# Asking for the square of a Mamba block's result one block later

## The chip, the cores and the metric

The kernel runs on one core of one Trainium2 chip. The time is the device time of one execution in microseconds, taken three times; 4633.89 us is the median.

## The reference, cut to what matters

Two layers over 32 graphs of 512 nodes with 256 features. Each layer normalises, adds an attention over the graph's edges, normalises again and adds a second part: in layer 0 a Mamba-2 block over the 512 nodes, in layer 1 an LSTM along the node axis with two running sums. The lines that the change concerns are the end of the Mamba block:

```python
Y = (Y_diag + Y_off + xh * D[:, None]).reshape(Bsz, L, D_INNER)
Y = Y * jax.nn.silu(z)
Y = Y * jax.lax.rsqrt(jnp.mean(Y * Y, axis=-1, keepdims=True) + EPS) * norm_w
out = Y @ W_out
return out @ W_lin + b_lin
```

`D_INNER` is 512. The mean of `Y * Y` goes over all 512 channels of a node.

## The kernel before, in words

Everything but the LSTM is done graph by graph ("batch" below), by generators that each issue a few instructions and then yield. Several of them run side by side, shifted against each other: `mamba` on graph b, `mamba_in` and `mamba_dt` for the next one, `plain1` (the second attention, then `after1`, which stores the graph's result) on the graph before, `plain0` (the first attention) and `after0` (its normalisation) on graphs ahead. A loop at the end of `layers_per_batch` takes the generator whose due time comes first, so the code gives an order in which work is asked for. A scheduler then decides where each instruction stands in its engine's queue.[...] In the last two batches a further generator, `recurrence_weights`, prepares the LSTM's weights: POOL scales them in one tile `rwt`, SP's queue stores it to `wr`, and the next use of the tile (L1069, a memset of its last two columns) waits for that store. Four of the first eight stores have 128 rows and four have 127 (L1140). After the batches comes the LSTM (`recurrence`, 512 steps).

The Mamba block holds its 512 channels as four blocks (cc = 0 to 3) of 128 partitions by 512 nodes. For each block

- `decayed(cc)` makes g, the decay matrix of two heads: eight ACT operations (L760), one ACT exp over all of it (L764), one DVE product with C·B (L765). It is called one block ahead.
- PE adds up py from g and the inputs (L829), and from the carried states (L835).
- `finish(cc, py)` makes y = xh·D + py on DVE (L816), multiplies it by silu(z) (L817; on POOL for blocks 0 to 2, on DVE for block 3), and squares it on ACT into zs (L818). The tile zs held silu(z), which the square overwrites.

After the four blocks PE multiplies y by the joined output weights (po, L847), sums the squares (pss, L854), ACT copies the sums (ssr, L856), PE turns them into a column (psc, L859), DVE and POOL make the reciprocal root of it (L861, L54 and L56 through the helper `rstd_of`), and DVE adds the result into x (L865).

Beside this run, at the end of a batch: the last sums and results of `plain1` (pov L962, its scale rinv L967 and L969, ov L970 on ACT), `after1` (em: L874 on DVE, exp L875 on ACT; L877 and L878 on DVE; the store to X at L879), `after0` of another graph (L351 on ACT, L353 and L355 on DVE, L54, L56, L356 and L357 on POOL), and the layer norms of the next graphs: xn for `plain0` and xm for `mamba_in` (statistics L65 and L66, the offset L69 on DVE, the scaling L71 on ACT), their transposes pxT and pmT on PE (L279), and the copies of these on ACT (L282). POOL adds beta (L494) and blin (L605) to x once the norm has read it. At the start of a batch POOL multiplies ce by cT (L746) and adds bias0 to o (L593), which DVE reads at L341 before it makes xdt (L783); POOL then makes xdd (L793).

Of the kernel before, what the change touches and what calls it, by code (L numbers as in the profile page):

```python
# [13 lines left out]
AF = mybir.ActivationFunctionType  # L14
# [12 lines left out]
NC = DI // P  # L27
# [48 lines left out]
def layers_per_batch(ctx, tc, c, a, X3, odd=None, wr=None):  # L76
# [6 lines left out]
    nc = tc.nc  # L83
# [7 lines left out]
    def bank(name, pool=psr):  # L91
        return pool.tile([P, 512], F32, tag="bank", name=name)
# [589 lines left out]
    def mamba(b, state):  # L682
# [11 lines left out]
        zs = two.tile([P, NC, N], F32, tag="wide", bufs=4 if odd is not None else 3, name=f"zs{b}")  # L694
# [4 lines left out]
        xh = two.tile([P, NC, N], F32, tag="wide", bufs=4 if odd is not None else 3, name=f"xh{b}")  # L699
# [49 lines left out]
        def decayed(cc):  # L749


            bc = two.tile([P, 2, N], F32, tag="bc", name=f"bc{b}_{cc}")
            nc.sync.dma_start(
                out=bc.rearrange("p h l -> p (h l)"),
                in_=line[:, 2 * cc * N : 2 * (cc + 1) * N].to_broadcast([P, 2 * N]),
            )
            g = two.tile([P, NT, 2, P], F32, tag="g", name=f"g{b}_{cc}")
            for i in range(NT):
                for k in range(2):
                    nc.scalar.activation(  # L760
                        g[:, i, k, :], bc[:, k, i * P : (i + 1) * P], AF.Relu,
                        bias=cs[:, i, 2 * cc + k : 2 * cc + k + 1], scale=-1.0,
                    )
            nc.scalar.activation(g, g, AF.Exp, scale=-1.0)  # L764
            nc.vector.tensor_tensor(  # L765
                g, g, pcb.rearrange("p (i l) -> p i l", i=NT).unsqueeze(2).to_broadcast([P, NT, 2, P]), ALU.mult
            )
            return g
# [45 lines left out]
        def finish(cc, py):  # L814
            y = xh[:, cc, :]
            nc.vector.scalar_tensor_tensor(y, y, dcol[:, cc, :], py, ALU.mult, ALU.add)  # L816
            (nc.gpsimd if cc + 1 < NC else nc.vector).tensor_tensor(y, y, zs[:, cc, :], ALU.mult)  # L817
            nc.scalar.activation(zs[:, cc, :], y, AF.Square)  # L818

        for cc in range(NC):  # L820
            if cc + 1 < NC:
                ahead.append(decayed(cc + 1))
                yield
            g = ahead.pop(0)
            py = bank(f"py{b}_{cc}")
            for i in range(NT):
                for k in range(2):
                    h = 2 * cc + k
                    nc.tensor.matmul(  # L829
                        py[k * HD : (k + 1) * HD, i * P : (i + 1) * P],  # L830
                        xdt[:, i, h * HD : (h + 1) * HD], g[:, i, k, :],
                        start=(i == 0), stop=False,
                    )
            for i in range(1, NT):
                nc.tensor.matmul(  # L835
                    py[:, i * P : (i + 1) * P], came[:, i - 1, cc].rearrange("p two e -> p (two e)"), ce[:, cc, (i - 1) * P : i * P],
                    start=False, stop=(i == NT - 1),
                )
            finish(cc, py)
            yield  # L840
        pos = []
        for j in range(NT // 2):
            po = bank(f"po{b}_{j}")
# [158 lines left out]
    def each(*parts):  # L1002
        return stream([(b + at, b + until, make, b + n) for b in range(-2, nb + 1) for at, until, make, n in parts])

    streams = [
        each((0.0, 1.0, mamba, 0)),
        each((-0.097, -0.039, mamba_in, 0), (-0.026, 0.192, mamba_dt, 0)),
        each((0.55, 0.857, second, -1), (0.857, 1.52, first, 2)),
# [471 lines left out]
```

## Time and profile before

| what | value |
|---|---|
| three timed runs | 4614.34, 4633.89, 4634.27 us |
| their median | 4633.89 us |
| profiled execution, its own time | 4607.25 us |
| its span, first to last instruction | 4605.5 us |
| PE, DVE, ACT, POOL busy | 3910.5, 3345.0, 2957.3, 1275.3 us |
| mean granted clock of PE | 0.959 |
| starts of two ssr copies (L856), batches 5 and 6 | 672.01, 769.76 us |
| the same, batches 29 and 30 | 3020.75, 3154.71 us |
| first LSTM product | about 3303 us |

"Busy" is the time in which an engine executes. A group's or line's idle time is the idle time of the engine directly before those instructions, put down to the one whose signal came last. Idle time of an engine matters only if somebody later waits for what it did late. The granted clock is the share of full speed that PE was allowed. One batch takes about 97.5 to 98.4 us, so its end can be read on any of them; batch 5 is used, whose ssr copy starts at 672.01 us. A matmul on 32-bit data shows as two rows of the trace.

### The profile page before, as it was taken

To read this page: it belongs to the slowest core of one execution; us is meant where nothing else is said; L and a number is where in the kernel's file an instruction comes from. 1 tells how busy PE (TensorE), PEld (TensorE's weight loads), DVE (VectorE), ACT (ScalarE), POOL (GpSimd) and SP (SyncE) were. 2 spreads that over 40 slices of the span, in tenths; PEclk is the share of its full clock that TensorE was granted. 3 is DMA by queue.
4 is the path that set the end of the run, shared out by engine and by line. 5 is a ranking of instruction groups with operands and counts; after the bars stand their busy time and mean duration, and the time that the engine had idled before them with its cause. 6 is when DMAs were issued, how large, how long until landed. Compare 5 with 4: busy or idle time off the path is not lost. (4 is left out here: it accounts for less than half of the span.)

```text
span 4605.5 us, 116255 instructions
## 1 busy us (share of the span) xinstructions
PE 3910.5 (85%) x46798; PEld 2447.7 (53%) x46798; DVE 3345.0 (73%) x10429; ACT 2957.3 (64%) x6852; POOL 1275.3 (28%) x1371
## 2 busy tenths in 40 slices
PE   6888899988999888999888999867688888888883
PEld 3445554445554455544455544534466666666662
DVE  4676666676666776666766667745599999999997
ACT  4777777777777777777777777755344444444441
POOL 2333433334333334333334333344000000000000
PEclk8999999999999999999999999988899999999997
DMA  3111222121222212221112221221112222222225
GB/s 109 52 62 57 74 65 72 61 63 57 73 70 67 65 59 65 74 71 61 63 56 74 65 72 60 63 65 57 55 36 45 45 45 45 45 45 44 45 41 167
DMA packets 273755, 288.69 MB, mean 63 GB/s; under 512 B 151872, under 2 KB 224536, under 8 KB 271032
## 3 DMA queue, kind: packets, MB, share of 16 engines
q1 hardware_dynamic: 269832, 271.32, 20.8%
q10 hardware_dynamic: 3216, 9.81, 0.7%
q8 instruction: 371, 6.08, 0.6%
q14 instruction: 176, 1.44, 0.1%
q0 software_dynamic: 160, 0.04, 0.0%
HBM read 227.09 MB, written 37.11 MB: 57 GB/s over the span
## 5 line engine op out<-in xcount | busy, mean ns | idle before, releaser
L1267 PE MATMUL pg<-wall,h 128*32 128x96 f32 x16352 | 558.8, 276 | 176.8 <-DVE h L1349 169.3
L1267 PEld LDWEIGHTS pg<-wall,h 128*32 128x32 f32 x16352 | 374.1, 109 | 350.9 <-DVE h L1349 331.9
L1267 PE MATMUL pg<-wall,xTr 128*32 128x96 f32 (+1 forms) x16384 | 549.0, 274 | 0.0
L484 DVE SCALAR_TENSOR_TENSOR w<-w,adjT 128x1024 f32<-128x1024 f32 x256 | 348.5, 1382 | 249.2 <-ACT w L478 249.2
L1267 PEld LDWEIGHTS pg<-wall,xTr 128*32 128x32 f32 x16384 | 447.3, 110 | 5.0 <-issue 0.3
L710 DVE SCALAR_TENSOR_TENSOR acc<-px,convw,acc 128x511 f32<-128x511 f32 (+2 forms) x480 | 351.3, 744 | 84.6 <-ACT acc L705 76.8
L1326 ACT ACTIVATE z<-pg 128x96 f32<-128x96 f32 x512 | 128.7, 251 | 438.9 <-PE pg L1267 438.9
L478 ACT ACTIVATE w<-rb,neg,colsa 128x512 f32<-128x512 f32 x512 | 387.4, 807 | 8.0 <-PE psu L556 4.4
L746 POOL TENSOR_TENSOR ce<-ce,cT 128x384 f32<-128x384 f32 x128 | 185.2, 1476 | 658.6 <-ACT cT L718 654.9
L548 PE MATMUL pav<-w,hb 128*64 128x512 f32 x1024 | 351.8, 613 | 7.7 <-DVE w L484 4.6
L1337 ACT ACTIVATE z<-z 128x32 f32<-128x32 f32 x1024 | 234.7, 229 | 168.7 <-DVE z L1335 101.0
L829 PE MATMUL py<-g,xdt 128*64 128x128 f32 x2048 | 179.8, 315 | 179.2 <-DVE g L765 131.9
L760 ACT ACTIVATE g<-bc,cs 128x128 f32<-128x128 f32 x1024 | 324.4, 389 | 9.9 <-DMA bc<-line 6.6
L689 PE MATMUL px<-mT,win 128*128 128x512 f32 x640 | 305.1, 608 | 0.0
L54 POOL TENSOR_SCALAR ve<-mv 128x4 f32<-128x4 f32 x32 | 6.2, 194 | 1064.4 <-DVE mv L1191 1064.4
L56 POOL TENSOR_TENSOR rs<-ve,mhalf 128x4 f32<-128x4 f32 (+1 forms) x224 | 276.1, 1233 | 18.4
L847 PE MATMUL po<-wc,xh 128*128 128x256 f32 x1024 | 264.9, 404 | 4.6 <-DVE xh L817 2.5
L829 PEld LDWEIGHTS py<-g,xdt 128*64 128x64 f32 x2048 | 137.7, 157 | 236.3 <-DVE g L765 138.9
L1349 DVE STREAM_TRANSPOSE h<-hh 128x32 f32<-128x32 f32 x1024 | 216.4, 211 | 34.9
L689 PE MATMUL pz<-mT,win 128*128 128x512 f32 x512 | 240.4, 602 | 0.0
L962 PE MATMUL pov<-wb,wv 128*128 128x257 f32 x1024 | 236.5, 384 | 2.0 <-DVE wv L484 2.0
L1332 DVE SCALAR_TENSOR_TENSOR ab<-z 128x64 f32<-128x64 f32 x1024 | 226.7, 221 | 15.1 <-ACT z L1326 11.8
(249 smaller groups left out, 8539.6 us busy)
## 6 DMA issues: line engine op xcount, KB each, us to landing
bc<-line SPq DMA_DIRECT2D x128, 512.0 KB, 3.6
adj<-in_adj_dram SPq DMA_DIRECT2D x32, 1024.0 KB
rb<-linea SPq DMA_DIRECT2D x64, 512.0 KB, 5.0
ce<-line SPq DMA_DIRECT2D x64, 384.0 KB, 4.6
x<-in_x_dram SPq DMA_DIRECT2D x32, 512.0 KB, 6.5
X<-x SPq DMA_DIRECT2D x32, 512.0 KB
xt<-X SPq DMA_DIRECT2D x128, 128.0 KB, 2.1
x<-X SPq DMA_DIRECT2D x128, 128.0 KB, 3.5
```

Of the source, the lines that this page charges most:

```text
L56: nc.gpsimd.tensor_tensor(rs, ve, c.mhalf[:, :n], ALU.pow)
L478: nc.scalar.activation(w[:, t, k, :], rb[:, k, :], AF.Relu, bias=neg1, scale=cols[:, 2 * m + t, h + k : h + k + 1],)
L484: nc.vector.scalar_tensor_tensor(w[:, :, k, :], w[:, :, k, :], 1.0, edges, ALU.add, ALU.mult)
L548: nc.tensor.matmul(pa[k * HO : (k + 1) * HO, :], hb[:, j, 2 * q + k, :], w[:, t, k, :], start=(j == 0), stop=(j == NT - 1),)
L689: nc.tensor.matmul(pz, win[:, k, col : col + P], mT[:, k, :], start=(k == 0), stop=(k == DK - 1))
L710: nc.vector.scalar_tensor_tensor(acc[:, s:], pz[:, : N - s], convw[:, cc, k : k + 1], acc[:, s:], ALU.mult, ALU.add)
L760: nc.scalar.activation(g[:, i, k, :], bc[:, k, i * P : (i + 1) * P], AF.Relu, bias=cs[:, i, 2 * cc + k : 2 * cc + k + 1], scale=-1.0,)
L829: nc.tensor.matmul(py[k * HD : (k + 1) * HD, i * P : (i + 1) * P], xdt[:, i, h * HD : (h + 1) * HD], g[:, i, k, :], start=(i == 0), stop=F ...
L847: nc.tensor.matmul(po[:, i * D : (i + 1) * D], xh[:, cc, it * P : (it + 1) * P], wc[:, cc, :], start=(cc == 0), stop=(cc == NC - 1),)
L962: nc.tensor.matmul(po[:, : D + 1], ws[j // 2][:, j % 2, 0, it * P : (it + 1) * P], wb[:, j, :], start=(j == 0), stop=(j == NT - 1),)
L1267: nc.tensor.matmul(p[q * GB : (q + 1) * GB, :], lhs[k], w[:, k, q, s:e], start=(start and k == 0), stop=(stop and k == DK - 1),)
L1337: nc.scalar.activation(z[:, (10 + n) * H : (11 + n) * H], z2[:, 4 * n * H : (4 * n + 1) * H], AF.Tanh, scale=0.5)
```

## The change

`finish` no longer squares. A new small function `square(cc)` does, and it is called for block cc - 1 after block cc's sums and `finish`, and for the last block after the loop. The same 128 squares are made of the same data into the same place; the order in which they are asked for differs. All lines after it move down: L818 becomes L820, L829 becomes L831, L847 to L879 move by six.

```diff
             y = xh[:, cc, :]
             nc.vector.scalar_tensor_tensor(y, y, dcol[:, cc, :], py, ALU.mult, ALU.add)
             (nc.gpsimd if cc + 1 < NC else nc.vector).tensor_tensor(y, y, zs[:, cc, :], ALU.mult)
-            nc.scalar.activation(zs[:, cc, :], y, AF.Square)
+
+        def square(cc):
+            nc.scalar.activation(zs[:, cc, :], xh[:, cc, :], AF.Square)
 
         for cc in range(NC):
             if cc + 1 < NC:
...
                     start=False, stop=(i == NT - 1),
                 )
             finish(cc, py)
+
+            if cc:
+                square(cc - 1)
             yield
+        square(NC - 1)
         pos = []
```

## The prediction

> **What bounds it now.** I read the page first: span 4605.5 us, PE busy 85%, DVE 73%, ACT 64%. The recurrence fills 3299 to 4605.5 us and the edit does not touch it. The batches fill the rest, so I read the line of the square (L818), then one batch engine by engine, then the granted clock, then the stretch after 3020 us. The view of line L818 (instructions and durations, then the engine's idle time before them):
>
> ```profile
> L818 ACT ACTIVATE zs<-xh x128: 629/630/633, 161.5 to 3240.0; 128x512 f32<-128x512 f32 x128
> its engine sat idle before it (us, times) until:
>   POOL xh L817: 154.2, 67
>   DVE xh L817: 6.1, 3
> ```
>
> ACT loses 160.3 us in front of the squares. The timeline of batch 5's end shows whether anybody pays for that (start, length, engine, operation; in brackets the idle time before it and who ended it):
>
> ```profile
> 654.78 1.65 POOL L56 TENSOR_TENSOR rs<-ve,mhalf 128x8 f32<-128x8 f32 x1
> ...
> 654.44 0.63 ACT L818 ACTIVATE zs<-xh 128x512 f32<-128x512 f32 x1 [4.04 <-POOL xh L817]
> ...
> 655.69 1.06 ACT L764 ACTIVATE g<-g 128x1024 f32<-128x1024 f32 x1
> ...
> 656.46 0.69 DVE L355 TENSOR_TENSOR o<-o,rs 128x512 f32<-128x512 f32 x1 [3.60 <-POOL rs L56]
> ...
> 657.98 1.21 DVE L765 TENSOR_TENSOR g<-g,pcb 128x1024 f32<-128x1024 f32 x1
> ...
> 659.25 1.98 PE L829 MATMUL py<-g,xdt 128*64 128x128 f32 x16 [4.06 <-DVE g L765]
> ```
>
> PE's hole of 4.06 us ends with DVE's L765 on the last block's g. ACT's exp of that g (L764) is over at 656.75, but L765 starts only at 657.98, as DVE came to it late: L355 ahead of it waited until 656.43 for POOL's rs. So ACT's 4.04 us are not the last wait: even without them PE would start at 659.25. PE then runs without a gap of note to 676: py, po, pss, pra, psc, pmT. The one wait in it: po's sixth product needs the last block's L817 (DVE, done 664.94); its pair of rows starts at 665.00 and 665.32 where the 0.216 us spacing of the rows gives 664.69 and 664.91: 0.41 us.
>
> The granted clock by stretches (PE, PEld, DVE, ACT and POOL busy, clock, DMA share, GB/s):
>
> ```profile
> 655.70:659.00 3.30, 0.00 (x0) 0.00 (x0) 2.54 (x7) 2.42 (x4) 2.35 (x3) 1.00 0.00 0
> 659.10:662.40 3.30, 3.15 (x22) 2.83 (x23) 2.63 (x13) 2.68 (x5) 3.29 (x3) 0.50 0.10 20
> 662.50:665.90 3.40, 3.26 (x16) 2.57 (x15) 3.08 (x5) 3.18 (x6) 1.54 (x2) 1.00 0.75 286
> ...
> 751.30:754.50 3.20, 1.35 (x16) 0.98 (x12) 0.58 (x1) 2.27 (x4) 2.42 (x3) 1.00 0.00 0
> 754.70:761.30 6.60, 4.59 (x25) 4.03 (x26) 5.76 (x19) 5.39 (x9) 6.28 (x6) 0.50 0.27 88
> ```
>
> The hole costs twice: the clock is halved behind it, for 3.4 us in one batch and 6.8 in the next. Last, POOL and the waits between 3020 and 3155:
>
> ```profile
> 3095.85 0.10 POOL L1069 MEMSET rwt<- 128x2 f32 x1 [8.05 <-DMA wr<-rwt]
> ...
> 3106.53 0.10 POOL L1069 MEMSET rwt<- 128x2 f32 x1 [8.19 <-DMA wr<-rwt]
> 3106.59 2.48 POOL L593 TENSOR_TENSOR o<-o,bias 128x512 f32<-128x512 f32 x2
> ```
>
> ```profile
> DVE o L341 <- POOL o L593: 30.8, 1, 30.8
> ```
>
> There the weights of the recurrence stand in POOL's queue ahead of L593, and DVE (then PE, 31.25 us) waits. That batch takes 133.96 us where others take 97.5 to 98.4.
>
> **The change part by part.** Nothing is added or removed: 128 squares of 0.63 us, and 571 table loads in the built programs of both. Only places move, and I take them from the built order.
>
> *Block 0.* Its square, asked for a block later, is placed by the scheduler where it was: behind five L760 of block 3 and ahead of the other two, behind the same POOL L817. Some 28 waits of 4.04 us (113 of the 154) stay. Gain 0.
>
> *Blocks 1 and 2* go behind the last two ov (L970). ACT is free at 660.56; ov then runs 660.6 to 661.4 (0.46 each) instead of to 662.55. em (L874, DVE) can start at 661.5 rather than 662.58, so L816 of block 3 is no longer held by it to 663.19 but starts when py ends, about 662.75. L69 also leaves its place ahead of L817, where it waited for POOL until 664.17. L817 then ends at 662.75+0.74+0.1+0.7, about 664.2 rather than 664.94, and po's wait of 0.41 us is gone.
>
> *xn and xm.* L877 waits for em's exp (ACT, 663.0 to 664.06) and ends at 665.35 instead of 666.08. xn needs that; it runs 665.4 to 667.45, earlier by 1.1. PE's pxT moves ahead by one product of po: it comes up at 662.53+18x0.216 = 666.4 and needs the second xn at 666.46, its last at 667.4 against 667.45. I charge 0 to 0.1 us. xm falls behind xT, done at 670.6 instead of 669.06; pmT reads it at 674.83, so 4.2 us cover it. POOL does both L494 ahead of both L605, ending near 672.2 as before, and its next work comes at 674.20. L878 is 0.7 earlier, and X's DMA with it; SP's order in these batches is unchanged.
>
> So each batch of the 3.4 us kind is 0.41 us shorter at psc. What remains of it is a matter of the clock. [...] The starts of ssr (L856) lie 97.47, 97.73, 98.35 us apart, over and over; the sum, 293.55, is 86 windows of 3.413. PE resumes 84.71 after the last ssr, and from there to ssr takes 12.76 (resumed 0.2 behind a window's edge), 13.02 (2.2 behind) or 13.64 (0.9 behind). Half the cold stretch is lost, 1.6, 2.35 and 2.96, which leaves 11.16, 10.67, 10.68: only the first kind holds the wait, some 0.45. Without it a batch takes 95.38 plus the loss. From 0.22 behind the edge: 1.60, batch 96.98, next 1.63 behind: 2.60, batch 97.98, next 0.63: 3.10, batch 98.48, next 0.13. Sum 293.44: the same three kinds, the same 86 windows. The gain is handed back to the clock: 0. It is not 0 if 0.63 is on the short side; 0.60 was long in batch 1, and 0.40 short. Then mixed batches average 97.6, and 28 of them bring 6 us. I take 0, range 0 to -6.
>
> *The stretch after 3020.* Here the POOL and SP orders change. Before, POOL has eight L1069 ahead of L593; three of these wait some 8 us for a store of 127 rows (7.88, 8.05, 8.19). After, the four ce products (L746, held for ACT's cT until 3056.8) stand ahead of the first L1069, and L593 stands behind the seventh, with two such stores. Stepping with the old gaps: first L1069 at 3062.6, then 3067.3, 3072.1, 3075.6, 3079.2, 3089.8, 3100.5; L593 follows there instead of 3106.59: 6.1 earlier. One L1132 (0.72) splits its halves and four L1075 (1.4) precede xdd: 5.2 there. SP also issues rb ahead of wr<-rwt, where ACT waited 1.28 us for it and not 0.20: about 1 more. The eighth L1069 then sits ahead of vs (L54) and waits 8 us to 3112.6; L54 is due at 3121, so it is covered. Sum -6.5, between 0 and -10. In the last batch the moved squares meet no xn: 0 to 1.
>
> Sum: -6.5 from the profiled execution's 4607.25 gives 4600.8. That execution lies under all three timed runs (4614.34, 4633.89, 4634.27). On their median, 4633.89 - 6.5 = 4627.
>
> **Rivals.**
> 1. *It does what it says:* the squares no longer hold ACT. 28x4.04 = 113 us, 4521. Against it: the built order, and L765, which waits for DVE. 0.02.
> 2. *The clock's cycle breaks:* -6 more, 4621. For it: 0.63 lies close to the edge. 0.23.
> 3. *Slower: PE waits for xn.* pxT came forward by one product and has no slack in my sum. Whatever delays L877 or xn stops PE with all of po behind it, at 28 us in total per us. Beyond 1.06 us a batch it outweighs the 6.5 and 0.5%. With 1.3 (em's exp behind the fourth square, 0.63, and one 0.7 step of DVE): +36-6.5, 4663. Against it: L877 has lost L69's wait. 0.12.
> 4. *The stretch after 3020 gets worse:* one more 127-row store ahead of what DVE needs, +10.7, 4645. 0.08.
>
> **How the numbers follow.** The forecast (4627) has 0.55. What a measurement of this kernel can tell from no change is about 0.5%, 23 us; the three runs alone spread over 20. The range takes in the cycle's break, the lower of the two places where runs fall, and rival 4: 4598 to 4648. Faster by over 0.5% needs rival 1, or rival 2 with the runs falling low: 0.18. Slower is rival 3 with a remainder: 0.14. Within 0.5%: 0.68.
>
> **What would show it.** Right: ACT still idle near 4.04 before the first square, PE's hole of 4.06 ended by L765, po's pair evenly spaced, ssr's starts summing to 293.5 over three, L341's wait near 25 instead of 30.8. Wrong: idle time in front of pxT put down to ACT xn (rival 3), batches near 97.6 on average (rival 2), no PE hole (rival 1).

## The result and the profile after

| | median | lowest to highest | runs |
|---|---|---|---|
| before | 4632.80 us | 4603.65 to 4639.26 us | 13 |
| after | 4607.22 us | 4604.09 to 4611.98 us | 13 |

The ratio is 0.9966, with a 95% interval of 0.9950 to 0.9982: faster by 0.34%, which lies within the 0.5% that the forecast called no change. The ratio is taken over all the runs. The two medians alone differ by 25.6 us, which is 0.55%; the forecast had 6.5 us. The lists behind them say more. Before's 13 times fall into two groups, six at 4603.65 to 4619.44 us and seven at 4632.80 to 4639.26 us, with nothing between. All of after's lie where the lower group is. The two profiled executions, 4607.25 us before and 4607.65 us after, are both of the lower kind and do not differ. So there are two questions: what the change does inside an execution, and why the upper group is gone.

The view of the squares' line (L820 is L818 of before), instructions and then the idle time of ACT ahead of them:

```profile
L820 ACT ACTIVATE zs<-xh x128: 621/631/635, 159.5 to 3240.0; 128x512 f32<-128x512 f32 x128
its engine sat idle before it (us, times) until:
  POOL xh L817: 153.6, 65
  DVE xh L817: 15.6, 32
```

The wait on POOL is what it was (154.2 before), as block 0's square has not moved. Of the 15.6 us in 32 places, three waits were there before (two of 2.84 us in the last two batches, one in the first). New is that in the other batches the last square now waits for DVE's L817, 0.32 to 0.33 us in 28 of them, because ACT comes to it earlier. The timeline of the end of a batch, in the same columns as before:

```profile
652.32 0.63 ACT L820 ACTIVATE zs<-xh 128x512 f32<-128x512 f32 x1 [4.04 <-POOL xh L817]
...
652.66 1.65 POOL L56 TENSOR_TENSOR rs<-ve,mhalf 128x8 f32<-128x8 f32 x1
...
653.57 1.06 ACT L764 ACTIVATE g<-g 128x1024 f32<-128x1024 f32 x1
654.34 0.69 DVE L355 TENSOR_TENSOR o<-o,rs 128x512 f32<-128x512 f32 x1 [3.60 <-POOL rs L56]
...
655.86 1.21 DVE L765 TENSOR_TENSOR g<-g,pcb 128x1024 f32<-128x1024 f32 x1
...
657.13 1.97 PE L831 MATMUL py<-g,xdt 128*64 128x128 f32 x16 [4.07 <-DVE g L765]
...
662.28 0.63 ACT L820 ACTIVATE zs<-xh 128x512 f32<-128x512 f32 x1 [0.32 <-DVE xh L817]
```

It is the same picture as before: 4.04 us ahead of the square, 3.60 us ahead of L355, PE's hole of 4.07 us. Behind the hole po's products follow each other without the 0.41 us that PE had waited for L817. From PE's first product behind the hole to ssr a batch of the shortest kind takes 12.51 us instead of 12.76. The gain is 0.25 us, as pxT, one product further ahead, now finds the second xn not ready: two extra gaps of 0.17 and 0.06 us, where before had one of 0.05.

In the stretch after 3020 us the longest wait of DVE is, before 30.8 us, now:

```profile
DVE o L341 <- POOL o L593: 26.4, 1, 26.4
```

The batch there takes 128.58 us instead of 133.96. That this does not show in the profiled time is due to the batches ahead of it. Their mean, over 28 batches (the 2nd to the 29th of the trace's 32), rose from 97.85 to 98.13 us: 28 x 0.28 = +7.8 us, against -5.4 us in the stretch. Before's profile repeats 97.47, 97.73, 98.35. After's has 97.25, 97.84, 98.41 and, in three stretches, batches of 98.65 us. In these the clock is halved (granted 0.50) a second time, for 3.41 us, starting 58.9 to 59.6 us behind ssr, just behind a gap of only 1.28 us in PE's work at pxd (L780, waiting for DVE's L783). Here is the gap in one of these batches; its ssr starts at 1064.31 us, and the clock is halved from 1123.94:

```profile
1122.05 0.66 PE L780 MATMUL pxd<-ident,xh 128*128 128x128 f32 x4 [1.28 <-DVE xdt L783]
```

All 28 batches have this gap (1.28 to 1.29 us), in before's trace as in after's; a halved spell follows it in none of before's and in ten of after's.

That suggested a theory. In each trace all changes of the granted clock lie on one grid of 3.413 us (in before's, the first and the last halved spell start at 27.57 and 4539.99 us, 1322 steps apart, and every change between lies within 0.01 us of a step); a step of this grid is called a window, here and in the prediction. **Cycle theory:** a batch with a second halved spell takes 98.9 us in the kernel before, close to 29 windows (98.99). An execution that gets into it can stay there, and then it is one of the upper group. The change makes such a batch 98.65 us, which slips against the windows by a third of a microsecond per batch (ssr 2.48, 2.16, 1.82 and 1.49 us behind an edge in four that follow each other), so that it falls out again after three or four. The change is then faster because it can no longer stay in the slow cycle, not because of any wait that it removed. **The rival:** each batch gains a little (0.25 us or part of it), the stretch after 3020 us the rest, and the two groups are chance.

### The profile page after: what moved, and what is told of

It reads as the page before. It is cut to its first block, busy times and chain, and to the rows that moved or that the text cites. A ratio compares the mean times of both kernels' runs of the same rounds, so it can differ in the third digit from the quotient of the medians.

```text
span 4605.8 us, 116255 instructions
## 1 busy us (share of the span) xinstructions
PE 3919.1 (85%) x46798; PEld 2452.4 (53%) x46798; DVE 3362.5 (73%) x10429; ACT 2952.3 (64%) x6852; POOL 1299.5 (28%) x1371
## 5 line engine op out<-in xcount | busy, mean ns | idle before, releaser
L831 PE MATMUL py<-g,xdt 128*64 128x128 f32 x2048 | 177.1, 312 | 179.3 <-DVE g L765 132.1
L56 POOL TENSOR_TENSOR rs<-ve,mhalf 128x4 f32<-128x4 f32 (+1 forms) x224 | 292.3, 1305 | 18.4
L831 PEld LDWEIGHTS py<-g,xdt 128*64 128x64 f32 x2048 | 134.9, 154 | 239.3 <-DVE g L765 138.5
L853 PE MATMUL po<-wc,xh 128*128 128x256 f32 x1024 | 255.4, 401 | 2.0 <-POOL xh L817 1.1
```

Source lines behind the costliest of these rows:

```text
L56: nc.gpsimd.tensor_tensor(rs, ve, c.mhalf[:, :n], ALU.pow)
L831: nc.tensor.matmul(py[k * HD : (k + 1) * HD, i * P : (i + 1) * P], xdt[:, i, h * HD : (h + 1) * HD], g[:, i, k, :], start=(i == 0), stop=F ...
L853: nc.tensor.matmul(po[:, i * D : (i + 1) * D], xh[:, cc, it * P : (it + 1) * P], wc[:, cc, :], start=(cc == 0), stop=(cc == NC - 1),)
```

## The experiments

In the tables "second spells" counts, of the 28 batches of the one execution that was traced, those in which the clock is halved at pxd as well. The sets of runs come from different chips; a "before" is always the kernel before on the same chip as the runs beside it.

**The kernel before, traced twice more.** No edit.

> The kernel before once more, for its trace. Its 13 timed executions lie in two groups, 4604 to 4619 and 4633 to 4639 us; this look and the next ask what the upper group does. Clock theory (the groups are two ways in which the batches fall on PE's clock windows): if the look falls in the upper group, its batches are 98.9 to 99.0 us long (29 windows of 3.413 are 98.99) instead of 97.85 on average, nearly all the way through, with a second halved spell per batch near the pxd transposes; the batch after 3020 us stays at 134. In the lower group: 97.47, 97.73, 98.35 as in the first trace. Rival (the groups come from the stretch after 3020 us, where POOL waits for the stores): the batches stay at 97.85 in both groups, and the upper group's last-but-one batch takes about 160 instead of 134 us.

> The same kernel and the same question as before_look1; a second look, since one look falls in either group. Clock theory: whichever group the first fell in, an execution 25 to 30 us above another has batches about 1.0 us longer and an equal stretch after 3020 us. Rival: equal batches, and the difference after 3020 us.

The first of the two executions took 4629.45 us, in the upper group, the second 4610.97 us. The view of ssr's line over seven starts shows the cycle. First the execution that was profiled before the prediction, then the first of the two new ones:

```profile
L856 ACT COPY ssr<-pss x7: 586/586/586, 2042.3 to 2629.4; 128x512 f32<-128x512 f32 x7
```

```profile
L856 ACT COPY ssr<-pss x7: 585/585/585, 2060.7 to 2654.6; 128x512 f32<-128x512 f32 x7
```

Six batches take 587.1 us in the one and 593.9 us in the other: 97.85 and 98.98 us each. In the new one all 28 batches have the second spell. They begin at 98.87 us, creep up within a dozen batches to 98.98 to 99.00, which is 29 windows, and stay there to the end. What holds them there can be read from the trace. A batch shorter than 29 windows makes the next ssr start earlier behind its window's edge (2.25 us behind it at first, 1.61 at the end), and the earlier it starts, the longer PE takes from ssr to the end of the main hole: 86.12 us at first, 86.24 at the end. So the batch can stretch by 0.12 us, and the 0.11 us from 98.88 to 98.99 is just within that. After's 98.65 us would need 0.34. In the other new execution the 21 batches up to 2334 us are of the short cycle, and the last seven are of the long one: 99.06, 99.00, 98.99 and so on. So the upper group is the long cycle, 28 x (98.98 - 97.85) = 31.6 us at most, and an execution can change into it on its way. The profile that the prediction was made from held none of it.

**Each half of the change alone.** The squares are asked for later only in the batches ahead of the last three, or only in the last three (the edits stand against the kernel after):

```diff
-            if cc:
-                square(cc - 1)
+            if b < nb - 3:      # the second kernel: b >= nb - 3
+                if cc:
+                    square(cc - 1)
+            else:
+                square(cc)
             yield
-        square(NC - 1)
+        if b < nb - 3:          # the second kernel: b >= nb - 3
+            square(NC - 1)
```

> The change in all batches but the last three, which keep the old order; POOL's and SP's order after 3020 us is that of before. Clock theory: from PE's resumption to ssr 12.51 us at the shortest, as after the change, so no batch of 29 windows can repeat; one group of times, at the changed kernel's plus what its stretch after 3020 gains (134.0 - 128.6 = 5.4): about 4612, ratio to before 0.994 to 1.000 by how many of before's executions fall in its upper group. Rival (groups come from the stretch after 3020): two groups as before, 4605 and 4634.

> The change in the last three batches alone; all others keep the old order. Clock theory: two groups as before, each lower by the 5.4 us of the stretch after 3020: about 4600 to 4613 and 4628 to 4634; profile with 12.76 us from resumption to ssr and a last-but-one batch of 128.6. Rival: one group near 4605.

| | median | lowest to highest | runs | ratio to before |
|---|---|---|---|---|
| before | 4624.53 us | 4599.72 to 4636.35 us | 23 | |
| in all but the last three batches | 4610.28 us | 4607.37 to 4614.06 us | 12 | 0.9971 (0.9954 to 0.9987) |
| in the last three | 4625.94 us | 4607.62 to 4631.15 us | 12 | 0.9995 (0.9978 to 1.0013) |

The first has one group, as after has; ten of its 28 batches have the second spell, again three or four in a row. The second has two groups, four runs at 4607.62 to 4614.00 and eight at 4623.32 to 4631.15 us. Its trace, of an execution of 4610.33 us, goes over into the long cycle at the 17th batch and stays. So the change in the steady batches takes the upper group away, and that in the stretch after 3020 us does not. What the last part does is seen in its wait, first for the kernel changed in all but the last three batches, then for the one changed in these alone:

```profile
DVE o L341 <- POOL o L593: 30.7, 1, 30.7
```

```profile
DVE o L341 <- POOL o L593: 26.8, 2, 26.1
```

**The square of block 0 left out.**

```diff
-            nc.scalar.activation(zs[:, cc, :], y, AF.Square)
+            if cc:
+                nc.scalar.activation(zs[:, cc, :], y, AF.Square)
```

> The kernel before, with the square of block 0 (its zs) left out of every batch; the norm's sum then reads an old buffer and the output is not the reference's. It asks what ACT's wait of 4.04 us ahead of that square is worth. My theory: nothing, because PE's hole ends with DVE's L765, which is held by L355's wait for POOL. The hole stays at 4.0 to 4.1 us ended by L765, the batches stay between 97.2 and 98.7 us, and the time is between 4595 and 4615 us (or up to 4635 if batches of 98.99 us come in). Rival (the wait was a cost, and the change fails only because block 0's square stays where it was): the hole closes to under 1 us and 28 batches lose 4 us each, so about 4500 to 4530 us.

Measured: 4620.50 us (4598.76 to 4630.47, 10 runs), ratio 1.0001 (0.9972 to 1.0029). Its timeline, without any square ahead of L764:

```profile
657.50 0.69 DVE L355 TENSOR_TENSOR o<-o,rs 128x512 f32<-128x512 f32 x1 [3.60 <-POOL rs L56]
...
660.28 1.19 PE L830 MATMUL py<-g,xdt 128*64 128x128 f32 x16 [4.07 <-DVE g L765]
```

The hole is as long as ever, and L765 still ends it. ACT's 4.04 us are worth nothing, and a change that really moved block 0's square would have gained nothing by it. (Leaving the square out also made the scheduler move some other instructions behind the hole, among them one ov, xm, L69 and one L605, so only the hole is read from this run.) The two groups are there too (five runs at 4598.76 to 4615.39, five at 4625.61 to 4630.47 us): its batch with the second spell is 98.92 us long and grows to 98.98.

**The 0.25 us given back.** One of psc's four products is computed twice, which lengthens the chain behind ssr; nothing changes its place. Once on the kernel after, once on the kernel before:

```diff
-        for i in range(NT):
+        for i in (*range(NT), 0):
             nc.tensor.matmul(pst[:, i : i + 1], ssr[:, i * P : (i + 1) * P], quart, start=True, stop=True)
```

> The kernel after, with one product of psc computed twice, so about 0.22 to 0.25 us more in each batch's chain behind ssr; the moved squares stay moved. Cycle theory (the median fell because batches 0.25 us shorter no longer fit the slow cycle of 29 clock windows, 98.99 us, in which the kernel before can stay): 98.65 becomes about 98.88, as before, so the slow cycle is open again. The runs fall into two groups again, one at 4600 to 4620 us and one some 20 to 28 us above (4622 to 4634), though the moved squares are all still there. Rival (each batch simply gains 0.25 us by the change and loses it here): one group, 28 x 0.25 = 7 us above the kernel after, near 4614 us.

> The kernel before with the same extra product of psc. It controls for the product itself. Cycle theory: batches with the second halved spell become 98.88 + 0.23 = 99.11 us, longer than 29 windows (98.99), so they drift the other way, by 0.1 us and more per batch, and leave the slow cycle after at most some ten batches: no run of 98.99 us to the end, and one broad group between 4605 and 4640 us. Rival (the time is a plain sum): every run 7 us above the kernel before, so two groups near 4617 and 4641 us.

| | median | lowest to highest | mean of 28 batches | second spells |
|---|---|---|---|---|
| after, product twice | 4626.06 us | 4619.65 to 4630.68 us (12 runs) | 98.73 us | 20 |
| before, product twice | 4631.62 us | 4626.32 to 4635.95 us (12 runs) | 98.97 us | 24 |

The kernel before on this chip: 17 runs at 4598.76 to 4604.30, one at 4620.70 and 15 at 4626.19 to 4637.51 us. For the kernel after, 28 x 0.2 = 6 us of work brought about 19 us (4607.22 to 4626.06, on another chip, where the lower group of the kernel before lies some 9 us lower, so that the 19 is rather too small). That is the cycle theory's direction and not the rival's 4614. Its form was missed: I expected two groups and there is one, near the upper place. The trace shows why. The batch with the second spell is 98.85 us and creeps up to 98.99, but falls out after 12, 5 and more such batches, and comes back in four batches later each time. In the kernel before it is 99.10 us, too long by 0.11; it slips the other way, leaves after eight such batches at most, and comes back after one other. Here, too, the form was missed: one broad group from 4605 us on was expected, and all twelve runs lie near the upper place. The plain sum, two groups 7 us higher, is refuted as well.

**Taking the second spell away.** If the theory is right, PE needs only a little more to do ahead of it. The four transposes of the third part of pxd are issued twice, 4 x 0.11 us (the distance from one transpose's start to the next in after's trace):

```diff
-            for cc in range(NC):
+            for cc in (*range(4 if s == 2 else 0), *range(NC)):   # 1 instead of 4 in the third kernel
                 nc.tensor.transpose(
                     px[:, cc * P : (cc + 1) * P], xh[:, cc, s * P : (s + 1) * P], c.ident
                 )
```

> The kernel before, with the four transposes of the third part (s = 2) of pxd issued twice: 4 x 0.11 = 0.44 us of useless TensorE work in each batch, which ends up in the 1.28 us gap that PE has 57.7 us behind ssr; no other instruction changes its place. Cycle theory: in the window ahead of the second halved spell PE is busy 0.49 of the time; with 0.35 to 0.44 us more it is 0.59 to 0.62, the spell never comes, and the cycle of 98.99 us is closed, though the squares stand where they stood before. One group of runs, where the lower group of the kernel before lies (4598 to 4617 us), ratio to the kernel before 0.995 to 0.999 depending on how many of its runs are in its upper group. Rival (the gap is not what makes the slow cycle, or work on PE simply costs): two groups as before, or all runs up to 28 x 0.44 = 12 us later.

> The kernel after, with the same four transposes twice. Cycle theory: the kernel after loses its stretches of three or four batches of 98.65 us too; its batches repeat 97.25, 97.84, 98.41 (86 windows, mean 97.84) from the first to the last, 28 x (98.13 - 97.85) = 8 us less than the profiled execution of the kernel after: about 4600 us, and 5 to 7 us under the other kernel of this pair (the gain behind 3020 us), because the 0.25 us per batch is then handed back whole. Rival (the 0.25 us per batch is a gain): 28 x 0.25 = 7 us more than that, 12 to 14 us under the other kernel.

> The kernel before with only one of these transposes twice: 0.11 us of useless TensorE work a batch. Dose for the same theory: the window ahead of the second spell goes from 0.49 busy to 0.52. If the clock turns at about one half, this is enough: one group, the lower one. If the turn lies well above 0.52, two groups as before.

| | median | lowest to highest | ratio to before | mean of 28 batches | second spells |
|---|---|---|---|---|---|
| before, 4 more | 4599.97 us | 4596.90 to 4603.04 us (12 runs) | 0.9970 (0.9948 to 0.9992) | 97.93 us | 0 |
| after, 4 more | 4596.14 us | 4593.91 to 4600.93 us (12 runs) | 0.9963 (0.9941 to 0.9985) | 97.86 us | 0 |
| before, 1 more | 4628.78 us | 4600.71 to 4634.34 us (12 runs) | 1.0010 (0.9981 to 1.0038) | 98.99 us | 28 |

The kernel before on this chip: 19 runs at 4599.45 to 4606.60 and ten at 4629.80 to 4635.90 us. With four transposes more it has one group, without any change to its squares. A fair comparison of the clock needs two batches that lie alike on the windows, since in most batches of the short cycle (all 28 of before's first trace, 18 of after's 28) no spell comes at pxd anyway. In the trace of the kernel after, every batch whose ssr starts 1.81 to 2.55 us behind a window's edge has the second spell. With four transposes more, nine of its batches start 2.43 to 2.54 us behind an edge, and none has it. Here is one of each, with ssr 2.51 and 2.49 us behind an edge: the window with pxd's gap and the next one (start and end, length, then PE, PEld, DVE, ACT and POOL busy, and the clock behind POOL's). First the kernel after, then the kernel after with four more:

```profile
823.56:826.97 3.41, 1.66 (x7) 0.52 (x6) 3.41 (x5) 3.38 (x6) 2.18 (x3) 1.00 0.33 126
826.97:830.38 3.41, 3.41 (x4) 1.40 (x5) 2.74 (x6) 1.44 (x4) 1.88 (x2) 0.50 0.09 32
```

```profile
823.89:827.30 3.41, 2.09 (x11) 0.78 (x9) 3.41 (x5) 3.38 (x6) 2.18 (x3) 1.00 0.38 129
827.30:830.71 3.41, 3.41 (x14) 1.25 (x15) 3.28 (x8) 1.47 (x4) 1.84 (x2) 1.00 0.08 26
```

PE is busy 1.66 of 3.41 us in the one, and the next window runs at half clock, with four rows of matmuls in it; it is busy 2.09 us in the other, and the next window runs at full clock with fourteen. The kernel before with four more has only one batch in that place (1.85 us behind an edge), and it, too, has no spell. One more transpose is not enough; the expectation had left that open. It brought only 0.06 us (1.66 to 1.72 us of a window of 3.41, a share of 0.504), and the two groups stayed.

The pair with four more also answers what the change itself is worth, as no run of either lies in the upper group. After's batches repeat 97.23, 97.89, 98.43 and before's 97.47, 97.74, 98.35. They sum to 293.55 and 293.56 us, 86 windows. Over six batches, first the kernel before with four more, then the kernel after with four more:

```profile
L856 ACT COPY ssr<-pss x7: 586/586/586, 2042.8 to 2629.9; 128x512 f32<-128x512 f32 x7
```

```profile
L862 ACT COPY ssr<-pss x7: 585/585/586, 2040.4 to 2627.5; 128x512 f32<-128x512 f32 x7
```

Both take 587.1 us: the 0.25 us of every shortest batch is handed back whole. The medians differ by 3.8 us and the means by 3.0 (95%: 1.2 to 4.8, worked out from the 12 and 12 runs), where 5 to 7 were expected from the stretch after 3020 us, and 12 to 14 by the rival.

**Cutting PE's main hole.** On the kernel after, half of the sum L357 goes from POOL to DVE, so that POOL's rs comes earlier:

```diff
-            nc.gpsimd.tensor_tensor(x[:, r], x[:, r], o[:, r], ALU.add)
+            (nc.gpsimd if n else nc.vector).tensor_tensor(x[:, r], x[:, r], o[:, r], ALU.add)
```

> The kernel after, with the first half of the block's x += o (L357, n = 0) moved from POOL to DVE. It cuts into what my theory says sets PE's hole: POOL's rs, for which DVE's L355 waits, comes about 1.1 us earlier, while DVE gets 0.7 us of work more. Theory: PE's hole of 4.07 us is split into pieces of under 2 us, no halved spell follows it, and 28 batches lose 2.5 to 4 us each: 4495 to 4540 us, ratio near 0.98. Rival (DVE is the engine that sets the batch): the added 0.7 us lies on its path and the time is the same or up to 20 us more, 4605 to 4627 us.

Measured: 4647.93 us (4636.41 to 4656.67, 8 runs), ratio to the kernel before 1.0079 (1.0050 to 1.0108). Slower than either side had it. The timeline shows that the step I aimed at did happen, and what came late instead:

```profile
663.61 1.09 PE L831 MATMUL py<-g,xdt 128*64 128x128 f32 x16 [2.15 <-DVE g L765]
...
667.19 1.09 PE L831 MATMUL py<-g,xdt 128*64 128x128 f32 x16 [1.62 <-DVE g L765]
...
674.85 1.45 POOL L494 TENSOR_TENSOR x<-x,beta 128x512 f32<-128x512 f32 x1 [4.07 <-ACT xn L71]
...
676.66 1.02 POOL L56 TENSOR_TENSOR rs<-ve,mhalf 128x4 f32<-128x4 f32 x1
...
677.72 1.23 DVE L69 SCALAR_TENSOR_TENSOR off<-bnmv,rs 128x4 f32<-128x4 f32 x1 [2.46 <-POOL rs L56]
...
681.92 0.57 ACT L862 COPY ssr<-pss 128x512 f32<-128x512 f32 x1
```

The hole is split in two, and the products behind both run at full clock (1.09 us, where they took 1.97). But the scheduler put L494 ahead of the norm's L56 in POOL's queue. L494 waits 4.07 us for xn, the offset L69 waits for L56, xm (L71) waits for L69, and ssr stands behind xm on ACT. Most batches take 99.0 us, whether the clock is halved in them or not. The hole was not the last thing that was late, and what it is worth alone stays open. More TensorE work in that hole, as at pxd, was not tried.

## Why the prediction was right, and where it was not

- **Block 0's square stays, and its 4.04 us are worth nothing:** right. The wait is there after the change, and without the square the hole still ends with L765.
- **po's wait of 0.41 us goes:** right. The term that was mis-sized is the charge of "0 to 0.1 us" for pxT, which waited 0.22 us, 0.17 more than before. The gain is 0.25 us, not 0.41.
- **The gain is handed back to the clock:** right for the cycle that the profile held. The pair without second spells shows 293.55 us over three batches, at 97.23, 97.89, 98.43 where 96.98, 97.98, 98.48 were worked out. Rival 2, the cycle's break, did come, but to the worse side: after's profile has the 98.65 us batches in ten places, and its mean is 98.13 us and not 97.6.
- **The stretch after 3020 us, -6.5 us:** right in mechanism, but the term was nearly twice too large. L341's wait went from 30.8 to 26.4 us, and the batch is 5.4 us shorter in the two profiles. Over the traces with the old order there (seven, 129.47 to 133.96 us) and the new one (four, 126.27 to 128.58), without the kernels that leave out a square or move L357, the means differ by 3.5 us. The prediction's printed terms, 5.2 and about 1, also add to 6.2 and not 6.5.
- **The failed step** is "on their median, 4633.89 - 6.5 = 4627". It took the distance between the profiled execution and the median as something that the change would leave alone. It was a second cycle of the same kernel, and it was the only thing that the change removed in earnest. The signs were there: the times fell into two places 20 us apart, the profile stood for the lower one, and a loop that kept to 86 whole windows over three batches (293.55 us) might keep to another number; it did, to 29 over one (98.99). The prediction applied the lock to the batches that it saw and did not ask which other lengths could lock.
- **The other rivals:** PE's waiting for xn cost 0.17 us a batch and not 1.3; the stretch after 3020 us did not get worse.
- **A count:** the prediction has 571 table loads in both programs. Both traces show 195; that the number is the same in both holds.

So the forecast of no change that can be told held for what an execution of the common kind costs, while nearly all of the 25.6 us in the medians came from a cause that it did not name. That the measured ratio stayed within 0.5% is in part luck: it depends on how before's 13 runs happened to divide, six to seven. Against the six of the lower group alone, the kernel after is faster by 0.07% (means 4610.6 and 4607.3 us), and by the medians by 0.55%. Shown by experiment: that the long cycle is the upper group, that it needs the halved spell at pxd, that the change in the steady batches closes it, and that giving back 0.2 us opens it again. Only read from the traces, and not tested, is what lets an execution in. Without the extra product of psc, the spell comes in batches whose ssr starts about 1.6 to 2.5 us behind a window's edge; in the short cycle of the kernel before, one batch of three starts at 1.39 to 1.53 (its first trace), just outside.

The fastest version is the kernel after with four more transposes, 4596.14 us. It beats the kernel before on its own chip by 0.37%. It lies under the kernel after (4604.09 us and more), though that was measured on another chip; the batches' means, 97.86 and 98.13 us, say the same.

## What to carry to other kernels

If the times of a kernel fall into two places, take a profile of each before costing an edit: here the profiled execution (4607.25 us) was of the one and the median (4633.89 us) of the other. Here the loop's period kept to whole windows of 3.413 us of TensorE's clock, 86 over three batches or 29 over one. A saving of 0.25 us in every shortest batch was worth nothing in the first (587.1 us over six batches with it and without it), and took the loop out of the second, which cost 31.6 us at most; the first trace held nothing of the second. Where a spell at a clock of 0.50 followed a gap of 1.28 us in TensorE's work, work that is thrown away mended it: 0.44 us did, and 0.11 us did not.

## What was not expected of the hardware

The clock fell to 0.50 behind a gap of only 1.28 us in PE's work (ten of 28 batches in after's trace), in windows that PE filled by about half. PE's busy share of each window can be worked out from the matmul rows on the grid of the spells. In the 28 batches, in all traces but that with L357 moved, the halved spells at pxd came behind windows with shares of 0.485 to 0.505, and no window with 0.53 or more was followed by a halved one.

But the share alone does not decide. In the same batches 30 windows with shares of 0.479 to 0.505 were followed by a full one. The two windows below, of the kernel before and of the kernel before with one transpose more, are equally busy, with ssr 1.53 and 1.62 us behind an edge:

```profile
2881.11:2884.52 3.41, 1.72 (x7) 0.78 (x7) 3.38 (x6) 2.49 (x3) 2.18 (x4) 1.00 0.41 154
2884.52:2887.93 3.41, 3.41 (x20) 1.76 (x20) 2.69 (x8) 1.41 (x3) 0.89 (x1) 1.00 0.00 1
```

```profile
2215.35:2218.76 3.41, 1.72 (x7) 0.72 (x6) 3.38 (x6) 2.58 (x3) 2.18 (x4) 1.00 0.40 154
2218.76:2222.17 3.41, 3.41 (x5) 1.18 (x4) 2.60 (x7) 1.41 (x3) 0.96 (x1) 0.50 0.02 5
```

The second holds one transpose of 0.11 us more; whether transposes count like other products was not tested. Outside the 28 batches, at the start and behind them, windows with shares of up to 0.73 were followed by a halved one. So no threshold is shown.

Nor did one busy stretch of any kind end a halved spell. In the same batches and traces, halved windows in which PE was busy up to 0.873 of the time were followed by another halved one (112 of them), those with 0.878 and more by a full one (502). That goes with the main hole costing 3.4 us of half clock in one batch and 6.8 in the next. The share here says mostly how long behind the window's edge PE resumed, and the traces cannot tell the one from the other; outside the 28 batches this line does not hold either.
